# A macaron block with neighbourhood attention: a bank of scores moved behind another product, and the setup written out by hand

## The chip, the cores and the metric

The kernel runs on one core of one Trainium2 chip. The metric is the device time of one execution in microseconds (us). The engines of the core are named as in the profile: PE (TensorE: matmuls; PEld are its weight loads), DVE (VectorE), ACT (ScalarE), POOL (GpSimd), SP (SyncE, which issues nearly all DMAs here). Each engine works through its own list of instructions in order and waits at semaphores for the others.

## The reference

The input x has 4 x 4096 rows of 512. Three residual steps follow each other: half a feed-forward layer whose inputs and weights are rounded to a 6-bit grid with a scale per block of 32, attention of 16 heads in which each position sees its 13 neighbours, and the same feed-forward layer again. Cut to what matters:

```python
def _mx_quantize(t, eps=1e-30):          # blocks of 32, grid of fp6 e2m3, largest value 7.5
    scales = max(max|block| / 7.5, eps)
    return nearest_on_grid(blocks / scales), scales

def _L0_ffn_ref(x, weight, bias):
    xd, wd = dequantised(x), dequantised(weight)
    return xd @ wd.T + bias

def _L0_attn_ref(x, ...):
    q, k, v = x @ qkv_w.T + qkv_b        # q scaled by 32 ** -0.5
    attn = softmax(q . k[13 neighbours] + rpb)
    return (attn . v[13 neighbours]) @ proj_w.T + proj_b

x = x + 0.5 * _L0_ffn_ref(_layernorm(x), ffn_weight, ffn_bias)
x = x + _L0_attn_ref(_layernorm(x), ...)
x = x + 0.5 * _L0_ffn_ref(_layernorm(x), ffn_weight, ffn_bias)
```

## The kernel before

The rows are cut into 128 tiles of 128 rows; four tiles make a group (512 rows). A "product" is twelve matmuls into one PSUM bank: both factors are split into a high and a low half in 16 bits, and three of the four combinations are taken over four slices of 128 (`product`, L146, matmul at L151). Per tile there are four products: `pmf1` and `pmf2` (the two feed-forward halves, both shown as `pmf`), `pmv` (values) and `pmo` (output). Per group there are four attention items, one for each four heads, each with two products `pmqk` (queries, keys). So one tile and one item go together, with six products.

An item `m` (`softmax`, L421) computes its scores block by block: a block has 30 queries and 42 keys, an item has 16 to 18 blocks, each with eight small matmuls (four heads, two parts) of 32 x 32 weights. Six blocks fill a PSUM bank, three banks hold an item (`ps`, one buffer). VectorE adds the bias and the two sides (L462, L465) into `sf` and takes the maximum; POOL subtracts it, ACT exponentiates, VectorE sums, POOL multiplies; ACT and POOL split the result into `p`, SP transposes it into `pT`. `attend` (L492) multiplies `pT` with the values (`pv`, four matmuls per block, 126 rows by 32 columns).

Order: the kernel doesn't leave the steady part to a scheduler. Every stage is a Python generator; `begin(slot, stage, rank)` puts it at a place, `yield n, rank` puts its rest n places later, and `run_slot` runs the stages of a place by rank. A tile takes `STEP` = 7 places. Relative to its tile or item, in places: first feed-forward product F1 = 5, values V = 20, queries and keys QK = 38 and 39, scores SC = 42, `pv` PV = 59, output OUT = 93, second feed-forward product F2 = 12 later. On PE this gives a fixed order per item: `pmf`, scores, `pmo`, `pmqk`, `pv`, `pmqk`, `pmf`, `pmv`.

The setup stands ahead of that. The FFN weight `fw` comes in four blocks of 128 rows; for each, its block scales are found and the quantisation is done in float32 with exact splits (L745 to L770): VectorE takes the quotients and differences, POOL the products with the split scale (L755) and the product back (L766), ACT the casts; the high and low halves go through `dma_start_transpose` into `wt` (`put_weights`, L703). The other sixteen chunks of weights (four each of queries, keys, values, output) are loaded into `rows`; the sums of their squares (ACT, L658) give powers of two that scale them (`powers`, L670; `scales`, L795), and `put_scaled` (L781) scales and splits a chunk on ACT and VectorE through one of four `whl` buffers and transposes it. `attention_bias` (L813) makes one product `pmb` with the output weights. A normed tile goes into the values and query products by way of `hln` (one buffer, L292) and a transpose into `x2`, shown as `x<-hln`.

Up to `manual_schedule()` (L779) a list scheduler orders the setup's instructions; behind it the written order holds. The first three tiles' norms (EARLY = 3) lie in the scheduled part; the chunks' `put_scaled` begin at the places in L866, in the order of `chunks` (L650): values, output, then queries and keys in turn.

Of the kernel before, what the change touches and what calls it, by code (L numbers as in the profile page):

```python
# [26 lines left out]
F32 = mybir.dt.float32  # L27
# [37 lines left out]
def macaron_kernel(  # L65
# [69 lines left out]

    def tie_to_lower(t):

        nc.vector.scalar_tensor_tensor(t, t, BELOW_ONE, t, ALU.mult, ALU.min)
        ti = t.bitcast(I32)
        nc.vector.tensor_scalar(ti, ti, 1, None, ALU.bitwise_or)
# [276 lines left out]
    def softmax(m):  # L421

        b, g, c = item_of(m)
        j0, j1 = group_blocks[g]
        n = j1 - j0
        t = qk.pop(m)


        ps = ps_s.tile([P, 3, 2, 256], F32, tag="s", name=f"ps{m}")
        for i in range(n):  # L430
            q0, k0 = (KN + at - g * GT for at in span(j0 + i))
            q0 -= late(j0 + i)
            u, w = divmod(i, PSB)
            for part, sides in ((0, 2), (1, 1)):
                for h in range(4):
                    rows = slice(h * D, (h + 1) * D)
                    nc.tensor.matmul(  # L437
                        ps[rows, u, :sides, w * KN : (w + 1) * KN],
                        t[rows, 0, part, q0 : q0 + QR], t[rows, 1, :sides, k0 : k0 + KN],
                        start=part == 0, stop=part == 1,  # L440
                    )

        def pieces(i, e):

            while i < e:
                u, w = divmod(i, PSB)
                whole = max((e - i) // PSB, 1) if w == 0 else 1
                f = min(e, (u + whole) * PSB)
                yield slice(u, u + whole), slice(w, w + (f - i) // whole)
                i = f  # L450

        yield 1, 9
# [5 lines left out]
        for i, e in ((0, first), (first, last), (last, n)):  # L458
            for u, w in pieces(i, e):
                o = s4[:, u, w, :]  # L460
                bias = table[:, kind(j0 + i), c, :].unsqueeze(1).unsqueeze(1).to_broadcast(o.shape)
                nc.vector.tensor_tensor(o, p4[:, 0, u, w, :], bias, ALU.add)  # L462
        for u, w in pieces(0, n):
            o = s4[:, u, w, :]
            nc.vector.tensor_tensor(o, o, p4[:, 1, u, w, :], ALU.add)  # L465
# [12 lines left out]
        nc.vector.tensor_tensor(total[:, :n], total[:, :n], p_scale[:, :n], ALU.mult)  # L478
        yield 1, 4
        nc.gpsimd.tensor_tensor(s, s, bc(total[:, :n], KN), ALU.mult)  # L480
        yield 2, 8
        p = p_tile
        ph = p[:, :n, :KN]
        nc.scalar.copy(ph, s)
        nc.scalar.copy(p[:, :n, 2 * KN : KV], ph)
        yield 2, 4
        nc.gpsimd.tensor_tensor(p[:, :n, KN : 2 * KN], s, ph, ALU.subtract)  # L487
        pT = ptp.tile([P, MAXB, P], F16, tag="pT", name=f"pT{m}")
        nc.sync.dma_start_transpose(out=pT[:, :n, :], in_=p[:, :n, :].rearrange("p n k -> p (n k)"))
        probs[m] = pT  # L490
# [75 lines left out]

    def add_bias(t, b):
        nc.gpsimd.tensor_tensor(xs[t], xs[t], b, ALU.add)  # L568
# [30 lines left out]
    for t in range(NT):  # L599
        k = t * STEP  # L600
        begin(k - 18, one(load, t), 0)
        enlist(k - 10, t, "n1")
        if not 0 < t < EARLY:
            begin(k - 11, one(moments, k - 10, t, "n1"), 1)
        begin(k + F1, first_half(t))
        begin(k + V, values(t))
        begin(k + F1, one(add_bias, t, half_ffn_b), 8)
        at = out_slot(t)
        begin(at - 5, one(add_bias, t, after_b), 8)
        enlist(at + 2, t, "n3")  # L610
        begin(at, project_out(t, at + 2))
        begin(at + 6 if t < LAST else second_slot(t) - 2, one(add_bias, t, half_ffn_b), 8)
        begin(second_slot(t), second_half(t))
    for slot in together:
        if slot >= EARLY * STEP - 10:
            begin(slot, quantised_norms(slot), 1)
# [12 lines left out]
    with tc.tile_pool(name="setup", bufs=1) as sp, tc.tile_pool(name="scratch", bufs=2) as scr:  # L629
# [10 lines left out]


# [3 lines left out]
        first = min(slots)  # L645
        for slot in range(first, first + EARLY * STEP, STEP):
            run_slot(slot)
        for _ in quantised_norms(-10):
            pass
        chunks = (8, 9, 10, 11, 12, 13, 14, 15, 0, 4, 1, 5, 2, 6, 3, 7)  # L650
        for o in chunks:
# [3 lines left out]
        for o in (*range(4 * KC, 5 * KC), *chunks):  # L655
# [3 lines left out]
        ptb = ps_m.tile([P, 512], F32, tag="mm", name="ptb")  # L659
        nc.tensor.transpose(ptb[:, : 3 * KC], b12, ident[: 3 * KC, : 3 * KC])  # L660
        bT = sp.tile([P, 3 * KC], F32, name="bT")
        nc.vector.tensor_copy(bT, ptb[:, : 3 * KC])
        b2 = sp.tile([P, 3 * KC], F32, name="b2")
        nc.vector.scalar_tensor_tensor(b2, bT, 2.0 ** -8, bT, ALU.mult, ALU.mult)
        nc.vector.tensor_tensor(sq[:, : 3 * KC], sq[:, : 3 * KC], b2, ALU.add)
# [4 lines left out]
        def powers(lo, hi):  # L670
# [7 lines left out]
            nc.tensor.transpose(ptn[:w, :P], top5[:, lo:hi], ident)  # L678
            most = sp.tile([w, 1], F32, name=f"most{lo}")
# [3 lines left out]
            ones_w = sp.tile([w, P], F32, name=f"ones{lo}")  # L683
            nc.gpsimd.memset(ones_w, 1.0)
            pb = ps_m.tile([P, 512], F32, tag="mm", name=f"pb{lo}")
            nc.tensor.matmul(pb[:, :w], ones_w, diag, start=True, stop=True)
            e = sp.tile([P, w], I32, name=f"e{lo}")
# [10 lines left out]

        powers(4, 5)
        nc.vector.tensor_scalar(cf, down[:, 4:5], 0.5 / XS, None, ALU.mult)  # L700
        nc.gpsimd.tensor_scalar(half_ffn_b, half_ffn_b, 0.5, None, ALU.mult)
# [22 lines left out]
        for o in range(KC):  # L724
# [3 lines left out]
            )  # L728
        nc.vector.tensor_scalar(w_sc, w_abs, 1.0 / Q_MAX, None, ALU.mult)
        split_scale()  # L730
        nc.vector.scalar_tensor_tensor(w_abs, w_hi, -Q_MAX, w_abs, ALU.mult, ALU.add)
# [4 lines left out]
        split_scale()  # L736
        w_back = small("w_back")
        nc.vector.tensor_scalar(w_back, w_sc, up[:, 4:5], F8_SCALE, ALU.mult, ALU.mult)

        def large(name, o, dt=F32):  # L740
            return scr.tile(
                [P, NB, QB], dt, tag=name, bufs=3 if name == "wu_" else KC, name=f"{name}{o}"
            )

        for o in range(KC):  # L745
# [5 lines left out]
            qh, q0 = large("wqh_", o, F16), large("wq0_", o)  # L751
            nc.vector.tensor_tensor(qh, fwb, per(w_r), ALU.mult)
            for i, b in enumerate((w_hi, w_lo)):
                u = large("wu_", f"{o}_{i}")
                nc.gpsimd.tensor_tensor(u, qh, per(b), ALU.mult)  # L755
                nc.vector.tensor_tensor(fwb, fwb, u, ALU.subtract)  # L756
            nc.vector.tensor_tensor(q0, fwb, per(w_r), ALU.mult)
            nc.vector.tensor_tensor(q0, q0, qh, ALU.add)
            q0f = q0.rearrange("p n q -> p (n q)")
            tie_to_lower(q0f)  # L760
# [5 lines left out]
            nc.gpsimd.tensor_tensor(fwb, w8, per(w_back), ALU.mult)  # L766
            hl = scr.tile([P, 2, dim], F16, tag="whl", bufs=4, name=f"whlf{o}")
            nc.scalar.copy(hl[:, 0, :], fw[:, o, :])
            nc.vector.tensor_tensor(hl[:, 1, :], fw[:, o, :], hl[:, 0, :], ALU.subtract)
            put_weights(4 * KC + o, hl)  # L770

        for t in range(1, EARLY):
            moments(t * STEP - 10, t, "n1")
            for _ in quantised_norms(t * STEP - 10):
                pass

        ctx.enter_context(tc.manual_schedule())  # L779
# [15 lines left out]
        def scales():  # L795
            powers(0, 4)
# [68 lines left out]
        begin(0, one(scales), 9)  # L865
        for slot, o in zip((2, 4, 5, 6, 10, 13, 16, 19, 21, 23, 25, 27, 29, 31, 33, 35), chunks):  # L866
            begin(slot, put_scaled(o), 9)
        begin(28, attention_bias(), 9)
# [50 lines left out]
```

## Time and profile before

| | |
|---|---|
| median of three runs | 2388.48 us (2378.66, 2388.48, 2392.82) |
| the profiled execution | 2398.3 us, its span 2396.5 us |
| granted PE clock, mean | 0.99 |
| busy: ACT, POOL | 55%, 83% |
| DMA queue q1, share of 16 engines | 74.3% |
| product, small matmuls of an item's scores, of `pv` (starts apart) | 2.59, 1.22, 0.62 us |

"Busy" is the share of the span in which an engine executes. A line of the timeline has the start and the duration in us, engine, line of the kernel, operation, output <- inputs, shapes, count, and in brackets the idle time before it with what ended it. A line of the waits has: engine, what waited, what it waited for, total us, number, longest. "SPq" is the time a DMA takes to be issued on SP's queue; a line that begins with DMA in the chain of waits is a transfer from issue to landing. "issue" means that the profile shows nothing that the engine waited for.

### The profile page before, as it was taken

The numbers are of one execution on the slowest core, as the hardware profiler recorded it, in microseconds if no ns is written. First come the engines' busy times: TensorE is split into PE (matmuls) and PEld (weight loads), VectorE is DVE, ScalarE is ACT, GpSimd is POOL, SyncE is SP. The second block draws the span as 40 slices with busy tenths as digits, with TensorE's granted clock in tenths as the row PEclk, the third lists the DMA queues.
The fourth block names the chain that finished last, engine by engine and source line by source line (L and its number), as shares of the span: only waits on it lengthen the run. The fifth ranks groups of instructions, "written<-read, shape, count | busy, mean of one in ns | idle before, by whom it ended". The sixth has DMA issues, their size and how long they took to land.

```text
span 2396.5 us, 82360 instructions
## 1 busy us (share of the span) xinstructions
PE 2285.3 (95%) x35539; PEld 1118.5 (47%) x35539; DVE 2020.8 (84%) x3588; ACT 1329.8 (55%) x2080; POOL 1990.2 (83%) x2012
## 2 busy tenths in 40 slices
PE   0799999999999999999999999999999999999998
PEld 0344444444444444444444444444444444444443
DVE  8789888888888888888888888888888878888886
ACT  4466555555555555555555555555555555555542
POOL 5578888888888888888888888888888888888886
PEclk9899999999999999999999999999999999999999
DMA  5789788777777777777777778877777786777773
GB/s 153 143 151 155 159 164 159 159 148 151 150 155 158 158 142 150 148 155 156 164 147 149 148 159 161 156 159 146 150 151 158 158 158 131 149 150 152 137 116 108
DMA packets 925701, 360.59 MB, mean 150 GB/s; under 512 B 718876, under 2 KB 889752, under 8 KB 925336
## 3 DMA queue, kind: packets, MB, share of 16 engines
q1 hardware_dynamic: 924992, 354.79, 74.3%
q8 instruction: 278, 4.55, 0.8%
q10 hardware_dynamic: 344, 0.53, 0.1%
q14 instruction: 87, 0.71, 0.1%
HBM read 110.15 MB, written 67.29 MB: 74 GB/s over the span
## 4 chain that ended last, share of the span: by engine, by line
PE 92%; DVE 4%; issue 1%; DMA 1%; POOL 1%; ACT 1%; SPq 0%; DVEq 0%; POOLq 0%; ACTq 0%
PE pmqk L151 28%; PE pmf L151 26%; PE pmo L151 14%; PE pmv L151 14%; PE ps L437 7%; PE pv L507 3%; DVE fw L756 0%; DMA x<-hln 0%; DVE hlq L204 0%; DVE stn L180 0%; DVE whl L786 0%; DMA fw<-in_L_ffn_weight_dram 0%; DVE sc L239 0%; POOL yq L251 0%; DVE x L279 0%
## 5 line engine op out<-in xcount | busy, mean ns | idle before, releaser
L151 PE MATMUL pmf<-wt,xT 128*128 128x512 f16 x3048 | 703.2, 381 | 12.9 <-DMA xT<-hlq 10.3
L151 PE MATMUL pmqk<-x,wt 128*128 128x512 f16 x3072 | 709.3, 381 | 4.8 <-DMA x<-hln 4.6
L151 PEld LDWEIGHTS <-xT 128*128 128x128 f16 x3048 | 298.8, 98 | 377.1 <-DMA xT<-hlq 12.7
L151 PEld LDWEIGHTS <-wt 128*128 128x128 f16 x3072 | 290.6, 98 | 342.7 <-issue 10.4
L151 PE MATMUL pmo<-wt,ring 128*128 128x512 f16 x1536 | 360.5, 385 | 8.5 <-issue 8.5
L151 PE MATMUL pmv<-wt,x 128*128 128x512 f16 x1536 | 354.1, 380 | 4.9 <-DVE mvn L181 4.9
L246 POOL TENSOR_TENSOR yq<-yq,r 128x1024 f32<-128x1024 f32 (+1 forms) x141 | 246.7, 1750 | 131.1 <-DVE r L244 131.1
L568 POOL TENSOR_TENSOR x<-x,half_ffn_b 128x512 f32<-128x512 f32 x256 | 327.8, 1280 | 0.1
L279 DVE SCALAR_TENSOR_TENSOR x<-pmf,coef,x 128x512 f32<-128x512 f32 x256 | 179.7, 702 | 151.9 <-PE pmf L151 151.6
L534 ACT ACTIVATE ring<-pv 128x510 f16<-128x510 f32 (+8 forms) x224 | 82.6, 415 | 396.6 <-PE pv L507 396.6
L314 ACT CAST vt<-pmv 128x512 f16<-128x512 f32 x128 | 75.1, 587 | 389.2 <-PE pmv L151 389.2
L180 DVE BATCH_NORM_STATS2 stn<-x 128x6 f32<-128x512 f32 x384 | 265.4, 691 | 9.0 <-DMA x<-in_L_attn_x_dram 0.2
L251 POOL TENSOR_TENSOR yq<-q,sc 128x1024 f32<-128x1024 fp8e4 (+1 forms) x141 | 246.9, 1751 | 1.0 <-ACT q L249 1.0
L151 PEld LDWEIGHTS <-x 128*128 128x128 f16 x1536 | 150.7, 98 | 187.6 <-DMA x<-hln 5.4
L377 DVE SCALAR_TENSOR_TENSOR qk<-pmqk,qk_b,qk 128x512 f16<-128x512 f32 x256 | 190.7, 745 | 52.9 <-ACT qk L373 51.8
L151 PEld LDWEIGHTS <-ring 128*128 128x128 f16 x1536 | 141.6, 99 | 173.2 <-issue 19.9
L480 POOL TENSOR_TENSOR sf<-sf,total 128x714 f32<-128x714 f32 (+2 forms) x128 | 178.8, 1397 | 42.8 <-DVE total L478 22.9
L186 POOL TENSOR_SCALAR rsq<-mv 128x2 f32<-128x2 f32 (+1 forms) x141 | 130.0, 922 | 99.3 <-DVE mv L181 96.9
L249 ACT ACTIVATE q<-yq,nudge 128x1024 fp8e4<-128x1024 f32 (+1 forms) x141 | 150.3, 1066 | 112.0 <-POOL yq L246 103.8
L373 ACT ACTIVATE qk<-pmqk,qk_b 128x512 f16<-128x512 f32 x256 | 176.5, 689 | 52.2 <-PE pmqk L151 50.4
L233 ACT ACTIVATE yq<-x,nbq,rsq 128x512 f32<-128x512 f32 x254 | 193.6, 806 | 18.3 <-POOL nbq L192 17.6
L487 POOL TENSOR_TENSOR p<-sf,p 128x714 f16<-128x714 f32 (+2 forms) x128 | 192.8, 1506 | 0.1
(145 smaller groups left out, 3466.3 us busy)
## 6 DMA issues: line engine op xcount, KB each, us to landing
vs<-vd SPq DMA_DIRECT2D x144, 357.0 KB
x<-in_L_attn_x_dram SPq DMA_DIRECT2D x128, 256.0 KB
vd<-vt SPq DMA_DIRECT2D x128, 256.0 KB
out_dram<-x SPq DMA_DIRECT2D x128, 256.0 KB
vs<-vd SPq DMA_DIRECT2D x24, 378.0 KB
vs<-vd SPq DMA_DIRECT2D x24, 315.0 KB
rows<-in_L_attn_qkv_w_dram SPq DMA_DIRECT2D x12, 256.0 KB
xT<-hlq SPq DMA_TRANSPOSE x141
```

The lines of the kernel that those rows point to most:

```text
L151: nc.tensor.matmul(pm, lhs(a, c), rhs(b, c), start=(n == 0), stop=(n == 3 * KC - 1))
L180: nc.vector.bn_stats(st, xs[t])
L233: nc.scalar.activation(y[:, u], xs[t], AF.Identity, bias=nb[:, u : u + 1], scale=rs[:, u : u + 1])
L246: nc.gpsimd.tensor_tensor(yb, yb, bc(r, QB), ALU.mult)
L251: nc.gpsimd.tensor_tensor(yb, q8.rearrange("p u (n q) -> p (u n) q", q=QB), bc(sc, QB), ALU.mult)
L279: nc.vector.scalar_tensor_tensor(xs[t], pm, cf, xs[t], ALU.mult, ALU.add)
L373: nc.scalar.activation(t[:, s, 0, KN:], pms[s], AF.Identity, bias=bias)
L377: nc.vector.scalar_tensor_tensor(t[:, s, 1, KN:], pms[s], bias, t[:, s, 0, KN:], ALU.add, ALU.subtract)
L437: nc.tensor.matmul(ps[rows, u, :sides, w * KN : (w + 1) * KN], t[rows, 0, part, q0 : q0 + QR], t[rows, 1, :sides, k0 : k0 + KN], start=par ...
L480: nc.gpsimd.tensor_tensor(s, s, bc(total[:, :n], KN), ALU.mult)
L487: nc.gpsimd.tensor_tensor(p[:, :n, KN : 2 * KN], s, ph, ALU.subtract)
L568: nc.gpsimd.tensor_tensor(xs[t], xs[t], b, ALU.add)
```

## The change

It has two parts. In `softmax`, the scores of all items but the last two are cut at twelve blocks (two banks). The first twelve are computed and added as before; the rest are computed three places later with rank 7, which is behind `attend` (rank 6) of that place, and added one place after; what follows of the item is three places later, from the split into `p` on two.

In the setup, `manual_schedule()` comes first, so every instruction's place is written out. VectorE takes all products of the FFN weight, two weight blocks at a time, with the norms of the first three tiles and the squares of the other weights woven in between. The first five tiles (`SOON` = 5) begin their first product at places 5, 8, 11, 14, 17 instead of 5, 12, 19, 26, 33, and their values products eight places after that; the first five tiles are loaded at once. The chunks come in the order values, queries and keys, output. `attention_bias` begins at place 33 instead of 28, `scales` is spread over three places.

```diff
@@ softmax
-        for i in range(n):
...
+        def scores(i0, e0):
+            for i in range(i0, min(e0, n)):
...
+        def add(i0, e0):
...
+        cut = 2 * PSB if m < n_items - 2 else MAXB
+        scores(0, cut)
+        yield 1, 9
+        add(0, cut)
+        if cut < n:
+            yield 2, 7
+            scores(cut, n)
+            yield 1, 9
+            add(cut, n)
         yield 1, 2
...
         nc.gpsimd.tensor_tensor(s, s, bc(total[:, :n], KN), ALU.mult)
-        yield 2, 8
+        yield 1 if cut < n else 2, 8
@@ places
+    SOON = 5
+    def n1_slot(t):
+        if t < EARLY:
+            return t - 10
+        return t * STEP - 10 if t >= SOON else 4 * (t - EARLY) + 1
+    def first_slot(t):
+        return t * STEP + F1 if t >= SOON else 3 * t + F1
...
-        begin(k - 18, one(load, t), 0)
-        enlist(k - 10, t, "n1")
+        begin(k - 18 if t >= SOON else first_slot(0) - 23 + t, one(load, t), 0)
+        enlist(n1_slot(t), t, "n1")
...
-        begin(k + F1, first_half(t))
-        begin(k + V, values(t))
-        begin(k + F1, one(add_bias, t, half_ffn_b), 8)
+        begin(first_slot(t), first_half(t))
+        begin(first_slot(t) + (V - F1 if t >= SOON else 8), values(t))
+        begin(first_slot(t), one(add_bias, t, half_ffn_b), 8)
@@ setup
+        ctx.enter_context(tc.manual_schedule())
...
-        chunks = (8, 9, 10, 11, 12, 13, 14, 15, 0, 4, 1, 5, 2, 6, 3, 7)
+        chunks = (8, 9, 10, 11, 0, 4, 1, 5, 2, 6, 3, 7, 12, 13, 14, 15)
...
-        for o in range(KC):
+        def quantise(o):
             fwb = blocks(fw[:, o, :])
...
             nc.vector.tensor_tensor(qh, fwb, per(w_r), ALU.mult)
-            for i, b in enumerate((w_hi, w_lo)):
-                u = large("wu_", f"{o}_{i}")
-                nc.gpsimd.tensor_tensor(u, qh, per(b), ALU.mult)
+            yield
+            for b in (w_hi, w_lo):
+                nc.vector.tensor_tensor(u, qh, per(b), ALU.mult)
+                yield
                 nc.vector.tensor_tensor(fwb, fwb, u, ALU.subtract)
+                yield
...
-            nc.gpsimd.tensor_tensor(fwb, w8, per(w_back), ALU.mult)
+            yield
+            nc.vector.tensor_tensor(fwb, w8, per(w_back), ALU.mult)
...
+        step(norms[0])
+        both(0, 4)
+        step(norms[0])
+        for o in chunks[:4]:
+            square(o)
+        moments(n1_slot(1), 1, "n1")
+        both(0, 2)
...
+        both(2, 1)
+        step(norms[1])
+        both(2, 1)
+        step(norms[1])
+        step(norms[2], 5)
+        nc.vector.tensor_tensor(sq[:, : 3 * KC], sq[:, : 3 * KC], b2, ALU.add)
...
-        begin(0, one(scales), 9)
-        for slot, o in zip((2, 4, 5, 6, 10, 13, 16, 19, 21, 23, 25, 27, 29, 31, 33, 35), chunks):
+        begin(0, scales(), 9)
+        for slot, o in zip((3, 4, 5, 6, 12, 15, 18, 20, 22, 24, 26, 28, 29, 30, 31, 32), chunks):
             begin(slot, put_scaled(o), 9)
-        begin(28, attention_bias(), 9)
+        begin(33, attention_bias(), 9)
         begin(26, one(put_table), 9)
```

More of the change, by code (lines that the diff above doesn't have):

```diff
@@ L134, in blocks @@
         return t.rearrange("p (n q) -> p n q", q=QB)
[L136 to L144, printed above, removed]
     def product(pm, lhs, rhs):
@@ L429, in softmax @@
         ps = ps_s.tile([P, 3, 2, 256], F32, tag="s", name=f"ps{m}")
-        for i in range(n):
[L431 to L441, printed above, removed]
+        def scores(i0, e0):
+            for i in range(i0, min(e0, n)):
+                q0, k0 = (KN + at - g * GT for at in span(j0 + i))
+                q0 -= late(j0 + i)
+                u, w = divmod(i, PSB)
+                for part, sides in ((0, 2), (1, 1)):
+                    for h in range(4):
+                        rows = slice(h * D, (h + 1) * D)
+                        nc.tensor.matmul(
+                            ps[rows, u, :sides, w * KN : (w + 1) * KN],
+                            t[rows, 0, part, q0 : q0 + QR], t[rows, 1, :sides, k0 : k0 + KN],
+                            start=part == 0, stop=part == 1,
+                        )
         def pieces(i, e):
@@ L450, in pieces @@
                 i = f
-        yield 1, 9
         sf = sfp.tile([P, MAXB, KN], F32, tag="sf", name=f"sf{m}")
@@ L457, in softmax @@
         last = n - (1 if kind(j1 - 1) == 2 else 0)
-        for i, e in ((0, first), (first, last), (last, n)):
-            for u, w in pieces(i, e):
-                o = s4[:, u, w, :]
[L461 to L465, printed above, removed]
+        def add(i0, e0):
+            for i, e in ((0, first), (first, last), (last, n)):
+                for u, w in pieces(max(i, i0), min(e, e0)):
+                    o = s4[:, u, w, :]
+                    bias = table[:, kind(j0 + i), c, :].unsqueeze(1).unsqueeze(1)
+                    nc.vector.tensor_tensor(
+                        o, p4[:, 0, u, w, :], bias.to_broadcast(o.shape), ALU.add
+                    )
+            for u, w in pieces(i0, min(e0, n)):
+                o = s4[:, u, w, :]
+                nc.vector.tensor_tensor(o, o, p4[:, 1, u, w, :], ALU.add)
+        cut = 2 * PSB if m < n_items - 2 else MAXB
[7 more added lines that the diff above has]
+            add(cut, n)
         yield 1, 2
@@ L600, in macaron_kernel @@
         k = t * STEP
-        begin(k - 18, one(load, t), 0)
-        enlist(k - 10, t, "n1")
+        begin(k - 18 if t >= SOON else first_slot(0) - 23 + t, one(load, t), 0)
+        enlist(n1_slot(t), t, "n1")
         if not 0 < t < EARLY:
-            begin(k - 11, one(moments, k - 10, t, "n1"), 1)
-        begin(k + F1, first_half(t))
-        begin(k + V, values(t))
-        begin(k + F1, one(add_bias, t, half_ffn_b), 8)
+            begin(n1_slot(t) - 1, one(moments, n1_slot(t), t, "n1"), 1)
+        begin(first_slot(t), first_half(t))
+        begin(first_slot(t) + (V - F1 if t >= SOON else 8), values(t))
+        begin(first_slot(t), one(add_bias, t, half_ffn_b), 8)
         at = out_slot(t)
@@ L614, in macaron_kernel @@
     for slot in together:
-        if slot >= EARLY * STEP - 10:
+        if slot >= n1_slot(EARLY):
             begin(slot, quantised_norms(slot), 1)
@@ L639, in macaron_kernel, with load_rows @@
         nc.scalar.dma_start(out=rp[:, QR - 1 : QR - 1 + NREL], in_=rpb)
+        ctx.enter_context(tc.manual_schedule())
         rows = {}
         sq = sp.tile([P, 5 * KC], F32, name="sq")
[L645 to L649, printed above, removed]
-        chunks = (8, 9, 10, 11, 12, 13, 14, 15, 0, 4, 1, 5, 2, 6, 3, 7)
-        for o in chunks:
+        chunks = (8, 9, 10, 11, 0, 4, 1, 5, 2, 6, 3, 7, 12, 13, 14, 15)
+        def load_rows(o):
             w, i = (qkv_w, o) if o < 3 * KC else (proj_w, o - 3 * KC)
@@ L654, in macaron_kernel, with square @@
             nc.sync.dma_start(out=rows[o], in_=w[i * P : (i + 1) * P, :])
-        for o in (*range(4 * KC, 5 * KC), *chunks):
+        def square(o):
             src = fw[:, o - 4 * KC, :] if o >= 4 * KC else rows[o]
@@ L658, in macaron_kernel @@
             nc.scalar.activation(junk, src, AF.Square, accum_out=sq[:, o : o + 1])
[L659 to L665, printed above, removed]
+        for o in range(4 * KC, 5 * KC):
+            square(o)
         top5 = sp.tile([P, 5], F32, name="top5")
@@ L678, in powers @@
             nc.tensor.transpose(ptn[:w, :P], top5[:, lo:hi], ident)
+            ones_w = sp.tile([w, P], F32, name=f"ones{lo}")
+            nc.gpsimd.memset(ones_w, 1.0)
+            yield 1, 9
             most = sp.tile([w, 1], F32, name=f"most{lo}")
@@ L682, in powers @@
             nc.vector.tensor_scalar(diag, ident[:w, :w], most, 2.0, ALU.mult, ALU.mult)
-            ones_w = sp.tile([w, P], F32, name=f"ones{lo}")
-            nc.gpsimd.memset(ones_w, 1.0)
             pb = ps_m.tile([P, 512], F32, tag="mm", name=f"pb{lo}")
             nc.tensor.matmul(pb[:, :w], ones_w, diag, start=True, stop=True)
+            yield 1, 9
             e = sp.tile([P, w], I32, name=f"e{lo}")
@@ L697, in powers @@
             nc.vector.tensor_scalar(d, d, 23, None, ALU.logical_shift_left)
-        powers(4, 5)
-        nc.vector.tensor_scalar(cf, down[:, 4:5], 0.5 / XS, None, ALU.mult)
-        nc.gpsimd.tensor_scalar(half_ffn_b, half_ffn_b, 0.5, None, ALU.mult)
         def put_weights(o, hl):
@@ L728, in macaron_kernel, with step @@
             )
+        first = min(slots)
+        for slot in range(first, n1_slot(1)):
+            run_slot(slot)
+        for o in chunks:
+            load_rows(o)
+        ffn_power = powers(4, 5)
+        next(ffn_power)
+        nc.scalar.activation(half_ffn_b, half_ffn_b, AF.Copy, scale=0.5)
+        norms = {t: quantised_norms(n1_slot(t)) for t in range(EARLY)}
+        def step(g, n=1):
+            for _ in range(n):
+                next(g, None)
+        step(norms[0])
         nc.vector.tensor_scalar(w_sc, w_abs, 1.0 / Q_MAX, None, ALU.mult)
         split_scale()
+        next(ffn_power)
+        ptb = ps_m.tile([P, 512], F32, tag="mm", name="ptb")
+        nc.tensor.transpose(ptb[:, : 3 * KC], b12, ident[: 3 * KC, : 3 * KC])
+        bT = sp.tile([P, 3 * KC], F32, name="bT")
+        nc.vector.tensor_copy(bT, ptb[:, : 3 * KC])
+        b2 = sp.tile([P, 3 * KC], F32, name="b2")
+        nc.vector.scalar_tensor_tensor(b2, bT, 2.0 ** -8, bT, ALU.mult, ALU.mult)
+        step(norms[0])
         nc.vector.scalar_tensor_tensor(w_abs, w_hi, -Q_MAX, w_abs, ALU.mult, ALU.add)
@@ L736, in macaron_kernel @@
         split_scale()
+        step(norms[0])
+        for _ in ffn_power:
+            pass
         w_back = small("w_back")
         nc.vector.tensor_scalar(w_back, w_sc, up[:, 4:5], F8_SCALE, ALU.mult, ALU.mult)
+        nc.vector.tensor_scalar(cf, down[:, 4:5], 0.5 / XS, None, ALU.mult)
         def large(name, o, dt=F32):
-            return scr.tile(
-                [P, NB, QB], dt, tag=name, bufs=3 if name == "wu_" else KC, name=f"{name}{o}"
-            )
-        for o in range(KC):
+            return scr.tile([P, NB, QB], dt, tag=name, name=f"{name}{o}")
+        def quantise(o):
             fwb = blocks(fw[:, o, :])
@@ L749, in per @@
                 return bc(t[:, o * NB : (o + 1) * NB], QB)
-            qh, q0 = large("wqh_", o, F16), large("wq0_", o)
+            qh, q0, u = large("wqh_", o, F16), large("wq0_", o), large("wu_", o)
             nc.vector.tensor_tensor(qh, fwb, per(w_r), ALU.mult)
-            for i, b in enumerate((w_hi, w_lo)):
-                u = large("wu_", f"{o}_{i}")
-                nc.gpsimd.tensor_tensor(u, qh, per(b), ALU.mult)
+            yield
+            for b in (w_hi, w_lo):
+                nc.vector.tensor_tensor(u, qh, per(b), ALU.mult)
+                yield
                 nc.vector.tensor_tensor(fwb, fwb, u, ALU.subtract)
+                yield
             nc.vector.tensor_tensor(q0, fwb, per(w_r), ALU.mult)
+            yield
             nc.vector.tensor_tensor(q0, q0, qh, ALU.add)
+            yield
             q0f = q0.rearrange("p n q -> p (n q)")
-            tie_to_lower(q0f)
+            nc.vector.scalar_tensor_tensor(q0f, q0f, BELOW_ONE, q0f, ALU.mult, ALU.min)
+            yield
+            qi = q0f.bitcast(I32)
+            nc.vector.tensor_scalar(qi, qi, 1, None, ALU.bitwise_or)
             w8 = large("w8_", o, F8)
@@ L765, in macaron_kernel, with both @@
             )
-            nc.gpsimd.tensor_tensor(fwb, w8, per(w_back), ALU.mult)
+            yield
+            nc.vector.tensor_tensor(fwb, w8, per(w_back), ALU.mult)
             hl = scr.tile([P, 2, dim], F16, tag="whl", bufs=4, name=f"whlf{o}")
             nc.scalar.copy(hl[:, 0, :], fw[:, o, :])
+            yield
             nc.vector.tensor_tensor(hl[:, 1, :], fw[:, o, :], hl[:, 0, :], ALU.subtract)
             put_weights(4 * KC + o, hl)
[L772 to L779, printed above, removed]
+        ready = [quantise(o) for o in range(KC)]
+        def both(o, n):
+            for _ in range(n):
+                step(ready[o])
+                step(ready[o + 1])
+        step(norms[0])
+        both(0, 4)
+        step(norms[0])
+        for o in chunks[:4]:
+            square(o)
+        moments(n1_slot(1), 1, "n1")
+        both(0, 2)
+        step(norms[0])
+        step(norms[1], 2)
+        both(0, 3)
+        step(norms[0])
+        moments(n1_slot(2), 2, "n1")
+        both(0, 1)
+        for o in chunks[4:8]:
+            square(o)
+        step(norms[0])
+        both(2, 2)
+        both(0, 1)
+        for o in chunks[8:12]:
+            square(o)
+        step(norms[1], 2)
+        both(2, 2)
+        step(norms[1])
+        step(norms[2], 2)
+        both(2, 2)
+        step(norms[1])
+        for o in chunks[12:]:
+            square(o)
+        both(2, 3)
+        step(norms[2])
+        both(2, 1)
+        step(norms[1])
+        both(2, 1)
+        step(norms[1])
+        step(norms[2], 5)
+        nc.vector.tensor_tensor(sq[:, : 3 * KC], sq[:, : 3 * KC], b2, ALU.add)
         def put_scaled(o):
@@ L795, in scales @@
         def scales():
-            powers(0, 4)
+            yield from powers(0, 4)
             nc.vector.tensor_scalar(cp, sd[:, 2:3], sd[:, 3:4], 1.0 / XS, ALU.mult, ALU.mult)
```

## The prediction

> **What bounds the kernel now.** I read the page's busy shares first, then TensorE's waits, then the timeline of one steady item, then the timelines of the first 125 us.
>
> ```profile
> span 2396.5 us, 82360 instructions
> PE 2285.3 (95%) x35539; PEld 1118.5 (47%) x35539; DVE 2020.8 (84%) x3588; ACT 1329.8 (55%) x2080; POOL 1990.2 (83%) x2012
> q8 instruction: 278, 4.55, 0.8%
> PE ps L437 <- issue: 9.3, 7, 3.4
> PE pmo L151 <- issue: 8.5, 4, 4.7
> ```
>
> TensorE (PE) is busy for 95%, and its waits for other engines lie at the two ends. In between it waits only for "issue": 18 us in 11 waits on the first matmuls after, or inside, a burst of scores. Queue q8 shows what that is: 278 reads of 4.55 MB, 16.4 KB each, against PE's 71,078 instructions: 256 per read. Counted over the trace's PE rows, the issue gaps after 200 us all begin at the same place in a block of 256, so PE stands there until its next block of instructions has landed. A steady item:
>
> ```profile
> 1008.69 1.28 PE L437 MATMUL ps<-qk 32*32 32x84 f16 x136
> 1009.91 2.76 PE L151 MATMUL pmo<-wt,ring 128*128 128x512 f16 x12
> ...
> 1026.28 1.28 PE L437 MATMUL ps<-qk 32*32 32x84 f16 x136
> 1027.49 0.60 PE L151 MATMUL pmo<-wt,ring 128*128 128x512 f16 x2
> 1030.15 3.97 PE L151 MATMUL pmo<-wt,ring 128*128 128x512 f16 x10 [2.05 <-issue]
> ```
>
> From scores to scores 17.59 us, with nothing between: six products of 2.6, scores 1.22, values by probabilities (`pv`) 0.6. So VectorE (DVE), ScalarE (ACT) and GpSimd (POOL) are covered there. The second item starves: 2.05 us of gap and a slow product after it. Summed over the items, starts of scores further apart than 17.59 add 26 us to this execution.
>
> The start:
>
> ```profile
> 29.86 1.53 DVE L757 TENSOR_TENSOR wq<-fw,w_r 128x512 f32<-128x512 f32 x1
> ...
> 37.12 0.68 DVE L757 TENSOR_TENSOR wq<-fw,w_r 128x512 f32<-128x512 f32 x1
> 53.86 2.61 SPq L704 DMA_TRANSPOSE wt<-whlf  x2
> 55.18 3.23 DMA wt<-whlf
> 58.50 5.28 PE L151 MATMUL pmf<-wt,xT-10_160 128*128 128x512 f16 x12 [15.17 <-DMA wt<-whlf]
> 74.10 4.45 PE L151 MATMUL pmv<-wt,x 128*128 128x512 f16 x12 [4.90 <-DVE mvn L181]
> 107.18 5.34 PE L151 MATMUL pmqk<-x,wt 128*128 128x512 f16 x24 [1.01 <-DMA x<-hln]
> ```
>
> The same operation takes 1.53 us while POOL multiplies and 0.68 without (0.60 apart in a row). The last FFN weight transpose is issued at 55.18 and lands 3.23 later; the first product starts at 58.50. From 58.5 to 107.18, the first query product, PE has large gaps; after that it is nearly dense. So the start is worth what that point moves, corrected for products moved across it.
>
> **The change part by part: the start.** The built order of each engine is fixed now, so I follow it.
>
> (a) VectorE begins the FFN weight later: the FFN power's small operations and the first norm's scale stand ahead, 15.19 becomes about 18.8. Each of the four weight blocks then takes 10.55 units of 0.60: product by reciprocal, two products that POOL had, two subtractions, quotient, add, tie step, an or (0.55), product back, low part. 4 x 10.55 x 0.60 = 25.3, plus two statistics (1.6), three low parts (1.8) and two block maxima (2.2) woven in: 30.9, to 49.7. POOL's six norm products still share: four or five of them beside VectorE, 0.9 each (1.53 - 0.60), 4.1; ACT's casts at the end, 1.5. VectorE is done at about 55.3. Taking POOL's twelve products costs 12 x 0.60 = 7.2, which eats what the missing contention saves.
>
> (b) On PE the transpose and product that make the other weights' powers (L692, L701) stand before the first product. Statistics, maximum, transpose, maximum, diagonal, product (0.9, 0.16, 0.37, 0.27, 0.2, 0.55 in the rows, with hand-overs) from 55.3 give 58.2. First product 58.2 against 58.50: nothing gained.
>
> (c) From the first product's end (63.5) to the landing of its normed tile `x<-hln` the old trace has 10.3 us (63.7 to 74.0). Now the bias add of tile 0 stands behind tile 3's and 4's norms on POOL, and those behind the power chain on VectorE: 3.4 more, 77.2.
>
> (d) The five values products follow each other through one `hln` buffer (hlp has one): cast on ACT 0.6, the next weight chunk 0.65, that chunk's low part and `hln`'s on VectorE 0.7 + 0.65, the chunk's transpose issue 1.3 on SP, then 3.15 to land (issue 39.61, landing 42.79, alone): 6.6 to 8 with a load between, 4.6 for the last. Four of them: 77.2 + 25.7 = 102.9, last values product done at 105.5.
>
> (e) Six of the sixteen weight chunks stand behind this product's evacuation on ACT and VectorE. VectorE still has the bias table (1.0) and a block maximum ahead, so they reach SP from 109.9 on, and there the queue sets the pace: five chunk transposes (6.5), one load (0.6), one `xT` (1.3) before the last one, issued at about 118.3 and landed at 121.5. The output weights are the last four chunks now, and `pmb`, which reads them, stands on PE before the first query product. After this idle a product takes 4.45 to 5.3: query product at about 126.4, 19.2 later than 107.18.
>
> (f) Two values products (5.2) lie before that point which lay behind it. But VectorE is busy for 11.3 of the 11.6 us of an early item, 0.69 of them theirs, so the two items shrink by 2 x 1.0 to 5.2: I take 3.5. Start: 19.2 - 3.5 = +15.7. Low end +5: (a) 3 us sooner, chunks off the loop of (d) (4 x 1.3), all of 5.2 gained. High end +20: (a) 2 later, (f) only 2.0.
>
> **The steady part.** Scores become 96 + 40 matmuls, the 40 straight behind `pv`.
>
> Fetch: a read of instructions begins at the earliest some 300 instructions before PE runs dry; from that point to its landing the trace has a median of 2.95 us, 6.1 at 95%, 9.6 at most, and PE goes on 1.3 after. The shortest time for 300 instructions is now 272 of scores (1.22) and 28 of a product (3.0): 4.4 us. Afterwards it is 36 of scores, two products, `pv` and the 40 (0.2 + 5.2 + 0.6 + 0.4): 6.4. Folding the measured latencies over all places of an item gives 19.6 us of waits before and 9.1 after, 46%. Of this execution's 26 us, 14 go. Ends: 4 (the long latencies lie where the bursts are) and 26.
>
> The Trainium skill ("Runtime: NRT & Kernel Launch", section on instruction fetch mechanics) says that fetch is hidden, since the sequencer issues more slowly than blocks arrive. The rows above disagree; by the rule this term would be 0 and the sum 14 higher.
>
> Switch: from a full product to small matmuls, start to start is 309 ns where products follow at 216, and from small ones to a product 113 where small ones follow at 8. The trace has no small kind behind another. Bounds: 0, if it goes on as inside a burst, and 0.105 per item (113 - 8). It is nearest to a change of array shape, so I take 309 - 216 = 0.093; 126 items: +11.7.
>
> The skill's "TensorEngine Tiling (Array Packing)", Key Properties, says that a change of tiling mode drains the array. That speaks against the change: `pv` uses 126 rows by 32 columns, the scores 32 by 32, a fifth switch per item. By it the term is what I took, without it 0.
>
> The rest is moved, not added. VectorE's adds come as before in 504 and 210 columns. Everything behind them is three places later up to the multiplication, then two: `pT` is issued 5 us later, and attend had 14 us to spare (issue 1030.9, landing some 5 later, use 1050.4). On SP `pT` now stands behind `xT` and `hln`, not before. On VectorE the late adds delay the low parts of the queries by 1.2; their bank is asked for at 1021.0, when they had finished at 1018.0. On POOL the norm's product comes some 0.4 later. Cost 0 under PE's cover; without it up to 0.25 per item, 32 us.
>
> **Sum.** This execution took 2398.3 (span 2396.5 and 1.8 around it): + 15.7 + 11.7 - 14.0 = 2411.7. It is 9.8 above the median of the runs, 2388.48. Without starvation it would be 2372.3, so the median run has 16.2 of it, of which 46% stay, 7.5: 2372.3 + 15.7 + 11.7 + 7.5 = **2407**.
>
> **Rivals.** One, the start closes up: were `pmb` and the chunks not ahead of the queries, that point would stay at 107 to 110 and the start cost 0. For it: the old order brought fourteen chunks by then. Against it: the last chunks stand behind five values products, and (d) is a chain of single waits. 2407 - 15.7 = 2391. It decides if the last values product ends before 92. Two, the fetch wins on the other side of zero: no switch is paid and no wait is left, 2372.3 + 15.7 = 2388, not slower. For it, the window of 6.4 exceeds 95% of the latencies; against it, 6.4 is less than 6.1 + 1.3, and the switches that are in the trace all cost. It decides if scores to scores stays at 17.59. Three, both: 2373. Four, a new wait in each item, VectorE's being the likeliest at 15.2 busy of 17.6: + 32, 2439. That the change doesn't do what it says is out: the built order shows 96, `pv`, 40.
>
> **How the numbers follow.** 0.5% (12 us) is about what a measurement can tell here: the three runs span 14. Chances: forecast 0.55 (0.50 of it slower), rival one 0.17 (0.13 same, 0.04 faster), two 0.16 (0.12 same, 0.04 slower), three 0.06 faster, four 0.06 slower. Slower 0.60, same 0.30, faster 0.10. The forecast's own range is 2398 to 2418; to leave out no more than two in ten it reaches down to rival two, 2388.
>
> **What would show it.** First product near 58; `pmb` waiting for a DMA and the first query product near 126; scores to scores 17.68 instead of 17.59; "issue" waits on PE of some 10 us instead of 19, fewer behind scores. I am wrong if the query product comes before 112, if the item stays at 17.59, or if an item has a new idle on PE.

## The result and the profile after

| | median (range), us | runs |
|---|---|---|
| before | 2389.31 (2378.66 to 2393.68) | 6 |
| after | 2421.89 (2419.42 to 2425.04) | 6 |
| after / before | 1.0141, 95% interval 1.0117 to 1.0165 | |
| forecast | 2407, range 2388 to 2418 | |

The change costs 32.6 us. The direction was forecast; the size was 15 us short, and the measured time lies outside the range. The profiled execution of after took 2419.65 (span 2417.9, granted clock 0.989), 21.35 more than the profiled execution of before; the sum had given 13.4 more.

The page of after, to lay beside the lines shown of before:

```profile
span 2417.9 us, 82202 instructions
PE 2289.8 (95%) x35539; PEld 1123.7 (46%) x35539; DVE 2060.7 (85%) x3646; ACT 1324.8 (55%) x2081; POOL 1970.6 (82%) x1999
```

Its list of PE's waits (engine, what waited, for what; total us, number, longest):

```profile
PE pmb L141 <- DMA wt<-whl: 19.0, 1, 19.0
PE pv L514 <- DMA pT<-p: 18.5, 14, 4.8
...
PE pmv L141 <- DVE x L269: 9.8, 1, 9.8
```

The share of PE is the same 95%. What is new stands in the waits: "issue" is gone from the list altogether (19.2 us in before), and `pv` now waits 14 times for `pT`, which it did once for 0.5 us in before. The chain of waits of after has `DMA pT<-p` with 5% of the span.

PE's timeline of after, the points of the start that the prediction gave:

```profile
59.53 5.30 PE L141 MATMUL pmf<-wt,xT-10_324 128*128 128x512 f16 x12
...
80.24 5.30 PE L141 MATMUL pmv<-wt,x 128*128 128x512 f16 x12 [9.83 <-DVE x L269]
...
107.98 2.76 PE L141 MATMUL pmv<-wt,x 128*128 128x512 f16 x12 [0.27 <-DMA x<-hln]
129.70 4.75 PE L141 MATMUL pmb<-wt,vbx 128*128 128x512 f16 x12 [18.96 <-DMA wt<-whl]
134.29 5.34 PE L141 MATMUL pmqk<-x,wt 128*128 128x512 f16 x24
```

First query product at 134.29 instead of 107.18: 27.1 later, where 19.2 were forecast. A steady item of after:

```profile
1003.26 0.95 PE L429 MATMUL ps<-qk 32*32 32x84 f16 x96
...
1009.43 0.69 PE L514 MATMUL pv<-pT,vs 126*32 126x30 f16 x68
1010.05 0.49 PE L429 MATMUL ps<-qk 32*32 32x84 f16 x40
...
1020.94 0.95 PE L429 MATMUL ps<-qk 32*32 32x84 f16 x96
```

17.68 from scores to scores, with no gap: the change does what it says, at the price forecast.

Where the time went is seen by following the start of each item's scores, as after minus before in the two profiled executions: +24.5 at item 0, +22.2 at item 1 (the two values products that now lie ahead of it), then +31.1 at item 3, +25.5 at item 4, +32.9 at item 7, +33.2 at item 19, +26.8 at item 60, +22.1 at the last. So at item 1 the start has cost 22.2, where the forecast has 15.7 in the end; items 2 to 11 lose again what should have come back there; and from item 19 on the changed kernel gains 11 us on the old one, although each of its items is 0.09 longer. (That gain is one of these two executions: the profiled one of before is 9.0 above its median run.) Five of the 14 waits for `pT` lie at items 0, 3, 4, 7 and 11, 11.6 us together; the other nine, of 0.3 to 1.9 us, are spread over items 27 to 126, and the last of them was there before.

### The profile page after: what moved, and what is told of

It reads as the page before. It is cut to its first block, busy times and chain, and to the rows that moved or that the text cites. A ratio compares the mean times of both kernels' runs of the same rounds, so it can differ in the third digit from the quotient of the medians.

```text
span 2417.9 us, 82202 instructions
## 1 busy us (share of the span) xinstructions
PE 2289.8 (95%) x35539; PEld 1123.7 (46%) x35539; DVE 2060.7 (85%) x3646; ACT 1324.8 (55%) x2081; POOL 1970.6 (82%) x1999
## 4 chain that ended last, share of the span: by engine, by line
PE 82%; DMA 6%; DVE 6%; POOL 2%; ACT 2%; issue 1%; SPq 0%; POOLq 0%; ACTq 0%; DVEq 0%
PE pmqk L141 25%; PE pmf L141 24%; PE pmo L141 12%; PE pmv L141 12%; PE ps L429 6%; DMA pT<-p 5%; PE pv L514 3%; DVE sc L229 1%; DVE stn L170 1%; DVE qk L367 1%; ACT yq L223 0%; POOL yq L236 0%; POOL x L587 0%; DVE x L269 0%; DMA x<-hln 0%
## 5 line engine op out<-in xcount | busy, mean ns | idle before, releaser
L141 PE MATMUL pmo<-wt,ring 128*128 128x512 f16 x1536 | 353.2, 380 | 0.0
L190 ACT CAST hlq<-yq 128x1024 f16<-128x1024 f32 (+1 forms) x140 | 134.9, 964 | 166.5 <-POOL yq L241 159.0
L229 DVE TENSOR_REDUCE sc<-yq 128x32 f32<-128x1024 f32 (+1 forms) x140 | 156.1, 1115 | 71.1 <-ACT yq L223 70.9
L429 PE MATMUL ps<-qk 32*32 32x84 f16 (+1 forms) x17536 | 186.0, 187 | 6.3 <-DVE qk L367 3.9
```

Of the source, the lines that this page charges most:

```text
L141: nc.tensor.matmul(pm, lhs(a, c), rhs(b, c), start=(n == 0), stop=(n == 3 * KC - 1))
L229: nc.vector.tensor_reduce(sc, yb, AX.X, ALU.max, apply_absolute_value=True)
L429: nc.tensor.matmul(ps[rows, u, :sides, w * KN : (w + 1) * KN], t[rows, 0, part, q0 : q0 + QR], t[rows, 1, :sides, k0 : k0 + KN], start=par ...
```

## The experiments

In the diffs, `-` is the kernel named as the base. All times are medians with ranges; e1 to e4 ran beside a before of 2389.49 (7 runs), e5 to e8 of 2389.64 (29 runs), e9 and e10 of 2386.15 (17 runs). The ratio to that before stands behind each time with its 95% interval. It is not the quotient of the two medians and differs from it by up to 0.2%.

**e1 and e2: each half alone.** e1 is before with the new `softmax` (the cut). e2 is after without the cut:

```diff
-        cut = 2 * PSB if m < n_items - 2 else MAXB
+        cut = MAXB
```

> The kernel before with the new softmax alone (scores cut at twelve blocks), old setup. Theory A (the start loses, the cut gains later but its early items wait for pT): first scores at about 117.6 as before; two or three waits of pv for the DMA of pT among the first ten items, together 5 to 15 us with the slow products after them; from item 14 on scores to scores 17.68 instead of 17.59 (+10 over the run) and no issue waits on TensorE (some -17 in a median run). Time 2389 + 10 (5 to 15) + 11 - 17 = 2393 (2388 to 2400). Rival B (the cut is the loss): 2405 or more, with idle on TensorE in every item.

> The changed kernel with the cut taken back (all scores at one place), new setup. Theory A: first query product at about 134, first scores at 142; no wait for pT; the two value products that lie earlier give back 2 to 5 us; issue waits as in the kernel before. Time 2389 + 20 to 27 = 2413 (2408 to 2417). Rival B (the setup is neutral): 2389 to 2394.

e1: 2402.59 (2401.93 to 2404.60), ratio 1.0060 (1.0037 to 1.0083). e2: 2408.60 (2404.87 to 2415.90), 1.0087 (1.0052 to 1.0122). The losses add: 13.1 + 19.1 = 32.2, measured 32.6. The cut alone lost four times what the forecast gives it in a median run (11.7 of switch less 8.7 of fetch, 3.0). Its list of waits says where:

```profile
PE pv L524 <- DMA pT<-p: 20.8, 11, 4.6
```

It has no "issue" wait, as after has none. e1 thus shows the `pT` wait to belong to the cut and not to the late start. The setup's 19.1 agrees within its interval with the forecast of 15.7; its scores start 21.6 later at item 0 and 15.1 later from item 4 to item 19.

**e3: is it the early items?** After, with the cut from item 8 on only:

```diff
-        cut = 2 * PSB if m < n_items - 2 else MAXB
+        cut = 2 * PSB if 8 <= m < n_items - 2 else MAXB
```

> The changed kernel with scores cut from the ninth item on only (8 <= m). Theory A: no wait of pv for pT among the first eight items, so 8 to 15 us less than the changed kernel: 2410 (2406 to 2415). Rival C (the waits for pT are only a part of the backlog that the start leaves, and move elsewhere): within 4 us of 2422.

2407.83 (2406.20 to 2409.94), 1.0081 (1.0057 to 1.0105): 14.1 less than after, and 0.8 less than with no cut at all (e2), which is within the noise. The cut of the first eight items costs 14 us; the cut of the other 118 costs nothing measurable as a sum (e3 has 1.4 us of "issue" waits where e2 has 16.6, and 5.8 of `pT` waits where e2 has 0.4, beside the switches). Why the eight cost so much shows in SP's queue in after (start, duration of the issue) and in the chain of waits (start, issue to landing):

```profile
161.78 2.90 SPq L403 DMA_DIRECT2D vs<-vd  x6
164.79 5.18 SPq L496 DMA_TRANSPOSE pT<-p  x1
```

```profile
164.79 8.65 DMA pT<-p
...
207.84 8.58 DMA pT<-p
221.46 9.85 DMA pT<-p
...
271.81 10.54 DMA pT<-p
```

Item 0's `pT` lands at 173.44 and its `pv` starts at 173.48. The loads of the values (`vs`: here three of 315 KB and three of 21 KB, at later items mostly three of 357 KB) are issued immediately ahead of it, and the issue of the transpose behind them takes 5.18; at items 3, 4, 7 and 8 of after it takes 6.5 to 7.6, where items 1, 2, 5 and 6 take 2.0 to 3.0. In before the same loads come behind `pT`, its issue at item 0 takes 4.59 and it has 4.1 us to spare:

```profile
133.28 4.59 SPq L489 DMA_TRANSPOSE pT<-p  x1
137.97 1.24 SPq L205 DMA_TRANSPOSE xT<-hlq  x1
139.31 1.29 SPq L205 DMA_TRANSPOSE x<-hln  x1
140.65 2.92 SPq L413 DMA_DIRECT2D vs<-vd  x6
```

The same happens in every second item to the end of the run. Here are a steady item of after and, behind it, the item of before from which the prediction read 14 us to spare:

```profile
996.50 1.60 SPq L403 DMA_DIRECT2D vs<-vd  x3
998.21 6.61 SPq L496 DMA_TRANSPOSE pT<-p  x1
```

```profile
1030.95 3.13 SPq L489 DMA_TRANSPOSE pT<-p  x1
```

Over the whole traces, `pT` lands a median of 14.2 us ahead of its `pv` in before. In after it is 8.3 in the 61 items whose transpose stands behind that of `hln`, and 0.5 in the 63 items in which it stands directly behind the values' loads. A steady item just fits into that or waits for 1 us at most; an early item, which has less to spare, does not fit.

Two theories were left: that `pT` is simply two places later in items too short for it, or that it is late because it now stands behind the values' loads.

**e5: move the loads, not the cut.** e1, with the values' loads one place later, so that they are issued behind `pT` again:

```diff
-        begin(k + 6 * STEP + 4, one(load_stack, b, g, 0), 9)
-        begin(k + 7 * STEP + 4, one(load_stack, b, g, 1), 9)
+        begin(k + 6 * STEP + 5, one(load_stack, b, g, 0), 9)
+        begin(k + 7 * STEP + 5, one(load_stack, b, g, 1), 9)
```

> The kernel before with the cut, and with the values' loads (load_stack) issued one place later, so that pT's transpose stands on SP ahead of them and not behind. Theory E (what the cut loses in the first third is pT waiting on SP behind the values' loads: issue 7 to 8.7 us and landing up to 12 instead of 4.5): every pT issue near 2.7, no wait of pv for pT, time 2402.6 - 10 to 18 = 2388 (2383 to 2393); scores to scores 17.68. Rival F (pT is late because it is made two places later, whoever stands before it): within 4 us of 2402.6, waits of pv remain.

2388.55 (2385.33 to 2391.09), 1.0010 (0.9996 to 1.0023): 14.0 less than e1, and no different from before; the forecast's switch and fetch, +3.0 in a median run, lie within its interval of -1.0 to +5.5. Its SP queue at item 0 and item 1, and its PE waits:

```profile
149.88 3.67 SPq L506 DMA_TRANSPOSE pT<-p  x1
...
163.04 2.17 SPq L506 DMA_TRANSPOSE pT<-p  x1
```

```profile
PE pv L524 <- issue: 4.6, 8, 1.0
...
PE ps L439 <- issue: 4.4, 5, 2.2
...
PE pv L524 <- DMA pT<-p: 0.7, 1, 0.7
```

No `pT` issue takes longer than 3.67; the landing, median over all items, comes 4.51 after the issue (6.34 in e1, 5.30 in before). The first five items keep 2.3 to 3.3 us to spare, so the two places alone do fit. This decides for the queue order. It also brings the "issue" waits back: 9.0 us, 47% of the 19.2 of before.

**e6: the same move in after.** The same two lines.

> The changed kernel with the same move of the values' loads. Theory E: 2421.9 - 10 to 16 = 2409 (2404 to 2413), the same as the new setup without the cut (2408.6). Rival F: within 4 us of 2422.

2409.21 (2405.12 to 2412.30), 1.0101 (1.0080 to 1.0122): 12.7 less than after by the medians, 9.6 by the two ratios to before. What is left is the setup's loss (e2: 2408.60). `pT` waits 0.5 us once; the "issue" waits that after had lost come back with 7.4, so the wait for `pT` cost more than this difference.

**e7: does the place of the late scores matter?** e5 with the last bank in front of `pv` instead of behind it:

```diff
-            yield 2, 7
+            yield 2, 5.5
```

> As the first kernel of this job, with the 40 late score matmuls in front of pv and not behind it. If the price of a switch is one of small kind to small kind whatever the direction: from scores to pv 113 ns, item 17.68, time as the first kernel within 2 us. If it is a price of changing to the smaller array shape only: scores to pv at 8 to 30 ns, item 17.59 to 17.61, 8 to 11 us less than the first kernel.

2390.12 (2388.53 to 2395.07), 1.0014 (0.9999 to 1.0029): the same as e5. From scores to `pv` 106 ns pass start to start, and from `pv` to scores 113 ns in after, where matmuls of one kind follow each other at 4 to 8. Measured on two orders, the switch between two kinds of small matmul costs the same in both directions.

**e4: the order of the chunks.** After, with the output weights' chunks in their old order ahead of the queries' and keys':

```diff
-        chunks = (8, 9, 10, 11, 0, 4, 1, 5, 2, 6, 3, 7, 12, 13, 14, 15)
+        chunks = (8, 9, 10, 11, 12, 13, 14, 15, 0, 4, 1, 5, 2, 6, 3, 7)
...
-        begin(33, attention_bias(), 9)
+        begin(28, attention_bias(), 9)
```

> The changed kernel with the chunks in the old order (values, output, then queries and keys) and the output bias from place 28, so that pmb no longer waits for the last of the sixteen transposes. Theory A: pmb straight behind the last values product at about 111, first query product by 114 to 118 instead of 134; some of the 16 to 20 us come back as waits of the later query products for their own weights. Time 2422 - 10 to 16 = 2409 (2405 to 2413). Rival D (ScalarE, VectorE and SP have the same work to do before the third item whatever its order): within 4 us of 2422.

2414.12 (2412.62 to 2419.82), 1.0111 (1.0085 to 1.0138): 7.8 less than after, a gain short of the expected one. The first item starts 11 us sooner than in after (+13.4 against +24.5 on before); three of those are gone by item 7, and the `pT` waits are still there (17.6 us). The chunks' order is a part of the start's loss, not all of it.

**e8 and e10: which closeness costs.** e8 is e2 with the first five tiles at their old places. e10 is e2 with only the values products of tiles 1 to 4 at their old places, and the first products still close together (second diff):

```diff
-        return t * STEP - 10 if t >= SOON else 4 * (t - EARLY) + 1
+        return t * STEP - 10
...
-        return t * STEP + F1 if t >= SOON else 3 * t + F1
+        return t * STEP + F1
...
-        begin(first_slot(t) + (V - F1 if t >= SOON else 8), values(t))
+        begin(first_slot(t) + V - F1, values(t))
```

```diff
-        begin(first_slot(t) + (V - F1 if t >= SOON else 8), values(t))
+        begin(first_slot(t) + 8 if t == 0 else t * STEP + V, values(t))
```

> The new written-out setup without the cut, with the first five tiles at their old places (5, 12, 19, 26, 33; values fifteen places later). Theory G (drawing the tiles together puts two more values products and their one-buffer chain ahead of the first query product): that product by 120 instead of 131, time 2408.6 - 6 to 12 = 2400 (2396 to 2403). Rival H (the written order and the output weights last are to blame, wherever the tiles stand): within 4 us of 2408.6.

> The new setup without the cut, first products of the first five tiles close together, but the values products of tiles 1 to 4 at their old places (27, 34, 41, 48). What the closeness costs (18.3 us between 2408.6 and 2390.3) lies either in the chain of first halves through the one hln buffer, which puts conversions, statistics and transposes of five tiles ahead of the chunks of the other weights on ScalarE, VectorE and the SP queue, or in the values products and their evacuations. Chain: the chunks stay late, pmb still waits some 15 us or more for its chunks, the values products only fill later places: 2404 to 2410. Values products: the chunks come forward, pmb's wait falls to some 8 us as with the spaced tiles, and 2391 to 2395.

e8: 2390.30 (2385.18 to 2401.80), 1.0016 (0.9998 to 1.0034), 18.3 less than e2 (17 by the ratios), a larger gain than was expected of it. e10: 2407.70 (2405.90 to 2414.51), 1.0082 (1.0059 to 1.0106), as e2. PE's timelines, e8 first, then e10:

```profile
98.08 2.93 PE L141 MATMUL pmv<-wt,x 128*128 128x512 f16 x12
109.26 4.12 PE L141 MATMUL pmb<-wt,vbx 128*128 128x512 f16 x12 [8.26 <-DMA wt<-whl]
113.22 5.34 PE L141 MATMUL pmqk<-x,wt 128*128 128x512 f16 x24
```

```profile
95.62 4.14 PE L141 MATMUL pmv<-wt,x 128*128 128x512 f16 x12 [2.80 <-DMA x<-hln]
122.29 4.44 PE L141 MATMUL pmb<-wt,vbx 128*128 128x512 f16 x12 [22.53 <-DMA wt<-whl]
126.57 5.34 PE L141 MATMUL pmqk<-x,wt 128*128 128x512 f16 x24
```

With the tiles apart the first query product comes at 113.22. With the values products apart, but the first halves close, `pmb` waits even longer for its chunks (22.5), since less work stands ahead of it. It starts at 126.85 in e2, 122.29 in e10 and 109.26 in e8: of these 17.6 us the values products make 4.6 (and e10 is no faster than e2 for that, since they only come later), and the first halves drawn together, with the norms ahead of them, make 13.0. A first half here is the first feed-forward product of a tile with what follows it: statistics, casts, low parts and transposes, for all five tiles through one `hln` buffer. How much of that is the one buffer, and how much the queue and the engines, was not tried.

**e9: the parts that cost nothing, together.** e8 with the cut and with the loads moved as in e5.

> The new setup with the first five tiles at their old places, the cut scores, and the values' loads one place later: every part of the change except the two that cost. The parts alone were 2390.3 (setup with old places) and 2388.55 (cut with later loads) beside 2389.6 before. If they add, 2389.2 (2386 to 2392). If the cut still needs the places that the old setup's early items left (the first query product comes 6 us later in the spaced setup than before, the early items are as tight), pT waits come back in the first eight items: 2395 or more. If both gains add below zero because starvation ends (spread 5.8 us instead of 17.5) on a start that loses nothing in the median, 2384 or less.

2394.84 (2392.52 to 2398.20), 1.0035 (1.0021 to 1.0048). This is a miss: 8.7 above the before that ran beside it, where the medians of the parts alone stood at +0.7 and -1.1. No `pT` wait is behind it (0.7 us once). Its scores start 5.9 later than before's at item 0, and e8's 6.1; 8.3 to 9.1 us of `pmb`'s wait for its chunks are left in both. So the spaced setup probably costs some 6 us, which e8's interval of -0.5 to +8 us contains, and e8's median alone read too well. By the ratios the parts add to +6.2 (1.0016 and 1.0010), inside e9's interval of +5.0 to +11.5, so nothing beyond the sum of the parts is shown. No version tried beats before by a measurable amount.

## Why the prediction was wrong, point by point

**The step that failed** is the one that begins "The rest is moved, not added" and ends "Cost 0 under PE's cover". It let `pT` be issued 5 us later on the word of one steady row with 14 us to spare, and named `xT` and `hln` as what `pT` now stands behind on SP. Two things were overlooked. The values' loads moved ahead of `pT` as well, and they stretch its issue from 2 to 3 us up to some 5 to 8 in every second item. And the spare time of that row isn't that of the early items: in before's own trace the landing of `pT` comes only 4.1 us ahead of its `pv` at item 0, 3.7 at item 4, 5.6 at item 5. The runs put 12.7 (after against e6), 14.0 (e1 against e5) and 14.1 (after against e3) on this wait; by the ratios to the before beside each it is 9.6, 11.9 and 14.3. A new idle on PE was one of the prediction's own signs of being wrong. Rival four had the right kind, a new wait, but on VectorE and in every item; it came on SP's queue, in 14 of 128 items.

Taken away (e6), the kernel takes 2409.2, and the forecast, which had no such wait, was 2407. That the two lie so close is partly luck: the start cost 3.4 more than said (e2), and switch and fetch together 4.1 less (e5 at -1.1, where +3.0 was said), both within the noise. The other terms:

- **Start, +15.7 forecast:** e2 measures +19.1, interval 12 to 29, and its scores start some 15 later from item 4 to item 45 in its trace; right as a sum, but by luck, for its points were off in both directions. The last values product came at 107.98 instead of 102.9, `pmb` at 129.70 instead of 121.5, the query product at 134.29 instead of 126.4. Against it, more was given back: e2's query product is 24.2 late, its first scores 21.6 and its item 4 15.2, so 9.0 came back where 3.5 were forecast. In after the `pT` waits swallowed that gain.
- **(a) and (b), first product at 58.2:** 59.53, by another cause. VectorE's last operation for the FFN weight ended at 50.46, not 55.3, and the one behind it at 51.06; but then it waited 5.19 for ScalarE's cast into the one `hlq` buffer, which waited for the transpose out of it, and the maximum of (b) came only behind that, at 57.76:

```profile
49.71 2.61 SPq L716 DMA_TRANSPOSE wt<-whlf  x2
...
52.41 1.29 SPq L195 DMA_TRANSPOSE xT-9_408<-hlq-9_402  x1
...
55.60 0.62 ACT L190 CAST hlq-8_415<-yq-8_366 128x512 f16<-128x512 f32 x1 [4.72 <-DMA xT-9_408<-hlq-9_402]
...
56.25 0.69 DVE L194 TENSOR_TENSOR hlq-8_415<-yq-8_366,hlq-8_415 128x512 f16<-128x512 f32 x1 [5.19 <-ACT hlq-8_415 L190]
```

  The column of brackets is the idle time and what ended it: the transpose stands on SP behind the FFN weight's, lands at 55.5, and holds cast and low part up in turn.
- **The FFN weight by VectorE alone:** called a wash (58.2 against 58.50); e8, which keeps it and the written-out order, stands at +0.7 (-0.5 to +8), and its scores start 6.1 later in its trace, so a loss of some 6 is not excluded.
- **Rival one, the start closes up:** its condition (last values product before 92) did not occur in after, where the last one starts at 107.98, nor in e8, where the last one ahead of the query product starts at 98.08. What an earlier query product is worth, e8 shows by another way: 18.3, with the tiles apart.
- **Switch, +0.093 per item:** 0.09 (17.68 against 17.59). From `pv` to the scores behind it 113 ns pass, start to start.
- **Fetch, 46% of the "issue" waits left:** 47% in e5 (9.0 of 19.2), 39% in e6 and e9 (7.4 each), 44% in e7 (8.5); the kernels without the cut have 16.6 to 18.0 (e2, e8, e10). Right where `pT` is in time, but from one profiled execution of each kernel, and that of before has more such waiting than its median run (26 against 16.2 us in the prediction's sum). (The prediction's shortest time of 4.4 adds 1.22 and 3.0, which is 4.2.) With late `pT` none are left in after, e1 and e4, and 1.4 in e3; these have the values' loads at the old place too, and which of the two removes the rest was not separated.

The Trainium skill's "TensorEngine Tiling (Array Packing)", Key Properties, has a change of tiling mode drain the array. The 113 and 106 ns between two small kinds agree with it. "Runtime: NRT & Kernel Launch", on instruction fetch, has the fetch hidden; here the waits for it halve when a burst of 136 becomes 96 and 40 (19.2 us in before, 7.4 to 9.0 in e5, e6, e7 and e9), so in these kernels it isn't.

## What to carry to other kernels

When a step is moved, list every transfer that it is moved past on its queue, and take its spare time from the tightest item of the trace, the first ones of a pipeline above all, not from a steady one. A DMA on the critical path goes ahead of bulk loads on the same queue: here one place in the order of two lines was worth 10 to 14 us of 2400. Before a stage is brought forward at the start, see what the first long product waits for: here drawing five tiles together kept its weights back, and that was worth 18 us.

## What the runs showed of the hardware

- A DMA transpose issued right behind three to six loads, 1.0 to 1.1 MB together, on the same queue held SP for 4.3 to 8.7 us, median 6.65 (63 of the 128 items in after and in e1), and landed 7.5 to 12.3 after its issue began, median 10.1 to 10.2. Behind another transpose (61 items of each) it was 1.5 to 3.6, median 2.6, and landing after a median of 4.5. At items 0, 1, 4 and 5 of before, with two other DMAs between the loads and the transpose, it held SP for 4.6 to 5.7. Why the issue stretches so was not taken apart.
- The kernels with shorter bursts spread less from run to run: 5.6 us (after, 6 runs), 5.8 (e5, 11 runs), 7.2 (e6, 5 runs), 6.5 (e7, 11 runs), 5.7 (e9, 12 runs), against 15.0 and 17.5 (before, 6 and 29 runs), 16.6 (e8, 12 runs) and 8.6 (e10, 6 runs). That the fetch waits make the difference was not shown.
